# A three-layer graph network on one core: one product per pair for tiles 11 to 21, and 655 listed gathers a layer in place of 495

## The chip, the cores and the metric

The kernel runs on one core of one Trainium2 chip. The metric is the device time of one execution in microseconds (us). The engines are named as in the profile: PE (TensorE; PEld is its weight load), DVE (VectorE), ACT (ScalarE), POOL (GpSimd), SP (SyncE, which issues most DMAs). Each engine works through its own queue in order; an instruction that waits for a semaphore holds up everything behind it on that engine.

## The reference

6250 nodes with 128 features, 200,000 edges sorted by destination, destinations crowded towards low node numbers (6250·u², u uniform), sources uniform.

```python
def _sage_conv(x, src, dst, Wl, bl, Wr):
    agg = jax.ops.segment_max(x[src], dst, num_segments=x.shape[0])
    agg = jnp.where(jnp.isfinite(agg), agg, 0.0)
    return agg @ Wl + bl + x @ Wr
...
h = jnp.maximum(_layernorm(x, axis=-1), 0.0)
# three layers, 128 -> 256 -> 256 -> 128, each: h = leaky_relu(_sage_conv(h, ...), 0.01)
x = x + h
```

So for every node and layer the elementwise maximum over the rows of its in-neighbours is wanted, then two small matrix products.

## The kernel before

**Tiles and pairs.** The nodes stand in 50 tiles of 127. As sources, two tiles make a pair, so there are 25 pairs. As destinations, tiles 0 to 2, whose nodes have the most edges, are split into 8 "virtual" tiles whose rows have at most 64 edges each; the other 47 tiles stand for themselves. The destinations are in four groups (`GROUPS`, L94): group 0 is 20 tiles (30 to 49), group 1 the 8 virtual tiles, group 2 the 19 tiles 3 to 21, group 3 the 8 tiles 22 to 29.

**Products.** A neighbour's row is fetched by a matrix product: for a destination chunk and a source pair, a one-hot matrix (`one_hot`, L940: ACT, and in layer 0 DVE at L956 for some) picks one edge per destination node, PE multiplies it with the pair's rows kept as a high and a low half (`products`, L990), and DVE takes the maximum with the accumulator (`maxima`, L1007). A *narrow* destination tile ("n") takes one edge per pair: both source tiles of the pair add into one PSUM tile, then one maximum. A *wide* tile ("w") takes one edge per source tile: two PSUM tiles and two maxima. The matmuls are as many for either. Virtual tiles are wide and have beside that a second, narrow product per pair (`EXTRA`, "x", L100). A step is one chunk of one group against one pair: up to 8 tiles of columns in layer 0 (128 features), up to 4 in layers 1 and 2 (256 features). A full step has 8 matmuls of 512 columns.

**Lists.** Edges that find no place in a product are listed (`pick_rows`, `rank_rows`, `send_row`: up to 24 or 48 per node) and sorted by length, so that the q-th row of 128 nodes of a list needs at most `CAPS[k][q]` edges. In each layer class `Listed` (L1009) fetches them with indirect DMAs that POOL issues (`gather`, L1039), 128 rows each: 495 of them a layer, which is the sum of `CAPS`. ACT releases the indices (`let`, L1028) two steps ahead (`LEAD`), a ring of 8 tiles `g` takes the rows, DVE folds them (L1053, L1058), and SP stores the result in `best`.

**Order.** The steps of a layer are dealt into sweeps over the pairs (`SWEEPS`, L1179): layer 0 as groups (0), (1), (2 with 3); layer 1 as (0 with 1), (2 with 3); layer 2 as (0 with 1), (2), (3). The main loop (L1420) writes for each step t, to all engines' queues, what an agenda holds for t. For the gathers the agenda is made at L1278 to L1300: they are spread evenly over the steps from `t0` to `t1`, and the fold that needs them is planned `DELAY` = 8 or 6 steps later:

```python
        t0, t1 = max(b0 + 2, rows_at), end - 1 - SOON
...
                    plan(max(whens[i] - LEAD, 0), LET, lambda li=li, t=t: li.release(t))
                    plan(whens[i], GATHER, lambda li=li, t=t: li.gather(t))
                    at = max(at, whens[i] + (SOON if k == NL - 1 else DELAY[layer]))
                plan(at, MAXIMA, lambda li=li, t=t: li.maximum(t))
```

`rows_at` is the step by which the last tile's new rows are written: when a group's sweep and list are done, its tiles go one by one through class `Node` (L1065: an indirect DMA `agg` on POOL, transposes, the two products, the row stored into the next layer's table), and those of groups 2 and 3 fall into the first 33 steps of the next layer. No gather of a layer may run before its table is whole.

**Layer 0** carries besides that the making of the lists and of the one-hot indices for groups 1 to 3 ("chores": `late_rows` L1218, `late_lookups` L1237), spread over steps 0 to 82. 44 gathers (`EARLY`) of layer 0 are issued before the first step.

Of the kernel before, what the change touches and what calls it, by code (L numbers as in the profile page):

```python
# [42 lines left out]
P = 128  # L43
# [7 lines left out]
CB = 40  # L51
# [8 lines left out]
)  # L60
NEAR, FIRST = 20, 30
DEEP = (24, 24, 48, 24)
WINDOW = (48, 64)
# [6 lines left out]
def kernel(ctx: ExitStack, tc: tile.TileContext, x, src, dst,  # L70
# [31 lines left out]
    PLACE, HEAD = {}, []  # L102
    for units in GROUPS:
        HEAD.append(len(PLACE))
        for u in units:
            PLACE[u] = len(PLACE)
    NU = len(PLACE)

# [3 lines left out]

    TILES = [[tile_of(u) for u in units] for units in GROUPS]
    LISTS = GROUPS
    NL = len(LISTS)
# [28 lines left out]
    cols = dram.tile([P, T], I16, name="cols")  # L144
    IW = [(len(units) + sum(w == "w" for w, _ in units)) * P for units in PLANES]
# [3 lines left out]
    OW = [sum(w == "w" for w, _ in units) * P for units in PLANES]  # L149
    far = [dram.tile([P, NG, FW[k]], U8, name=f"far{k}") for k in range(len(GROUPS))]  # L150
# [356 lines left out]
    def flag_rows(us, S):  # L507
# [23 lines left out]
        one_less = slice(0, J - 1)  # L531
        if wide and us[0][1] >= NW:
# [17 lines left out]
    def pick_rows(k, i0, us, S):  # L550

        n, W, m = len(us), width_of(us), DEEP[k]
        whole = S(0, F32, n, W)
        nc.vector.tensor_copy(whole, rows_of(us)[:, :, :W])
        top = S(2, F32, n, m)
        for i in range(n):
            for o in range(0, m, 8):
                nc.vector.max(out=top[:, i, o : o + 8], in_=whole[:, i, :])  # L558
                if o + 8 < m:
                    nc.vector.match_replace(  # L560
                        out=whole[:, i, :], in_to_replace=top[:, i, o : o + 8], in_values=whole[:, i, :], imm_value=0.0
                    )
        nc.vector.tensor_scalar(picked[k][:, i0 : i0 + n, :], top, -float(LEAF), 0.0, op0=OP.add, op1=OP.max)
        there = S(0, F32, n, m)
        nc.vector.tensor_scalar(there, top, float(LEAF), None, op0=OP.is_ge)
        nc.vector.reduce_sum(left_n[k][:, i0 : i0 + n], there, axis=AX.X)

# [153 lines left out]
    def window_check():  # L721
        for i, (c0, c1, n) in enumerate(
            ((FIRST, NT, WINDOW[0]), (22, FIRST, WINDOW[1]), (VT, 22, 2 * CUT))
        ):
# [25 lines left out]
    def lookups(us, least, s, pool, tags=("v", "v8")):  # L750
# [9 lines left out]
        while i < n:  # L760
# [8 lines left out]
            nc.scalar.copy(part.rearrange("g (c k) -> g c k", k=P), p[:, :m, :])  # L769
            at = NV + PLANES[k].index(us[i]) if us[i] in EXTRA else GROUPS[k].index(us[i]) + (len(GROUPS[k]) if s else 0)  # L770
            nc.sync.dma_start(idx[k][:, at * P : (at + m) * P], part)
# [59 lines left out]
    list_consts()  # L831
    for i0 in (0, NEAR // 2):
        mask_rows(L0[i0 : i0 + NEAR // 2], S_first)
        flag_rows(L0[i0 : i0 + NEAR // 2], S_first)
        if i0:
# [3 lines left out]
            for i in range(NW):  # L839
                row(("w", i))  # L840
        pick_rows(0, i0, L0[i0 : i0 + NEAR // 2], S_first)
    rank_rows(0, S_first, first)
# [87 lines left out]
    def parts_of(k):  # L930

        units = PLANES[k]
        for w in "wnx":
            us = [i for i, u in enumerate(units) if u[0] == w]
            for i0 in range(0, len(us), HOT // P):
                yield us[i0], len(us[i0 : i0 + HOT // P]) * P, len(GROUPS[k]) if w == "w" else 0

    hots, gone, slots, turn_o = {}, {}, {}, [0]

    def one_hot(layer, k, g, c, w, odd, s):  # L940

# [6 lines left out]
        if layer == 0:  # L948
            at = of + (c + (odd if s else 0) + (NV if PLANES[k][c] in EXTRA else 0)) * P
        elif k == 0:  # L950
# [26 lines left out]
    def products(step, s, p):  # L977
# [3 lines left out]
        K = widths[layer] // P  # L981
        c0, pw, _ = next(q for q in parts_of(k) if q[0] <= c < q[0] + q[1] // P)
        hot = hots[layer, k, g, c0, s]
# [81 lines left out]
    class Node:  # L1065
# [28 lines left out]
        def merge(self):  # L1094
# [4 lines left out]
            self.m = node.tile([P, 2, P], F32, tag="mz", name="mz", bufs=2)  # L1099
            if self.k is None:  # L1100
                nc.vector.tensor_copy(self.m[:, :K, :], aT_p)
# [79 lines left out]
    for layer in range(3):  # L1181
        begins.append(len(steps))
        for ks in SWEEPS[layer]:
            for g in range(NG - 1, -1, -1):
                kinds = [[], []]
                for k in ks:
                    for c0, w, _ in parts_of(k):
                        part = [c for c in chunks(layer, k) if c0 <= c[2] < c0 + w // P]
# [29 lines left out]
    def late_rows(k):  # L1218
        us = LISTS[k]
        i0 = 0  # L1220
        for part in [us]:
            chores.append((2.5, lambda part=part: mask_rows(part, S_acc)))
            chores.append((18 if part[0][0] == "w" else 6, lambda part=part: flag_rows(part, S_acc)))
            for i in range(0, len(part), 4):
# [47 lines left out]
    for layer in range(3):  # L1272
# [6 lines left out]
        alone = len(SWEEPS[layer][-1]) == 1  # L1279
        for part, t0, t1 in (((lists_[:3], t0, turn), (lists_[3:], turn, t1)) if alone else ((lists_, t0, t1),)):  # L1280
# [3 lines left out]
            n = sum(len(li.seq) for li in part) - early  # L1284
# [6 lines left out]
        done_at, i, at = [], 0, 0  # L1291
        for k, li in enumerate(lists_):
            for t in range(len(li.seq)):
                if whens[i] is None:
                    at = 1 + i // 8
                else:
                    plan(max(whens[i] - LEAD, 0), LET, lambda li=li, t=t: li.release(t))
                    plan(whens[i], GATHER, lambda li=li, t=t: li.gather(t))
                    at = max(at, whens[i] + (SOON if k == NL - 1 else DELAY[layer]))
                plan(at, MAXIMA, lambda li=li, t=t: li.maximum(t))  # L1300
                i += 1
            done_at.append(at)
        gap = (2, 3, 3)[layer]
# [59 lines left out]
    for i, (layer, sweep, g) in enumerate(order):  # L1363
        for k in SWEEPS[layer][sweep]:
            for c, w, odd in parts_of(k):
                for s in range(2):
                    jobs_h.append((at_step[layer, k, g, c], i, (layer, k, g, c, w, odd, s)))
    jobs_h.sort(key=lambda j: j[0])
# [33 lines left out]
    for t in range(EARLY):  # L1402
        soon.release(t)
        soon.gather(t)
    least = first.tile([P, len(L0), NG], I16, name="least_a")
    for g0 in range(0, NG, BATCH):
        expand(L0, CB, g0, 0, least, S_first)
    lookups(L0, least, 0, first, ("xs0", "xs1"))
    load_layer(0, const, first)
# [4 lines left out]
    made = making.enter_context(tc.tile_pool(name="made", bufs=1, side="right"))  # L1414
    acc_t = [work.tile([P, 2, n * P], F32, name=f"acc{i}") for i, n in enumerate((NN, NV + NW))]
    ACC = ((0, 0), (1, 0), (1, NV), (0, NEAR))
    pair_until(0)
# [326 lines left out]
```

## Time and profile before

| | |
|---|---|
| median of 3 executions | 3248.2 us (3247.44 to 3262.78) |
| the profiled execution | 3258.48 us; span from first to last instruction 3256.5 us |
| mean granted TensorE clock | 0.921 |
| busy share PE / DVE / ACT / POOL | 75% / 84% / 58% / 57% |
| DMA | 571.20 MB, mean 175 GB/s |

Busy time is that of instructions at work; POOL's time for a DMA is that of writing its descriptors, and the rows land later. A group's mean is the time of one instruction. "Idle before, releaser" says what ended the idle time ahead of it.

### The profile page before, as it was taken

What the parts mean: (1) busy time and instruction counts of PE and PEld (TensorE: products, weight loads), DVE (VectorE), ACT (ScalarE), POOL (GpSimd) and SP (SyncE); (2) the same over time, 40 slices, a digit from 0 to 9 for tenths busy, and PEclk for the clock granted to TensorE, in tenths of its full rate; (3) what the DMA queues carried; (4) which work ended last, traced back from release to release, by engine and by line L of the source; (5) the groups of instructions that cost most, each with busy time, mean ns of one, the idle gap of its engine ahead of it and who ended that gap; (6) DMA issues with size and microseconds to landing.
All of it is one profiled execution on the core that took longest, in us unless ns stands there. A gap on an engine that the chain in (4) does not pass through costs nothing.

```text
span 3256.5 us, 37116 instructions
## 1 busy us (share of the span) xinstructions
PE 2448.4 (75%) x9919; PEld 1785.3 (55%) x9920; DVE 2740.2 (84%) x4320; ACT 1901.7 (58%) x2753; POOL 1862.4 (57%) x1885
## 2 busy tenths in 40 slices
PE   1025622448777779999988888889999997878787
PEld 1023311235444457777765655567777775655566
DVE  6677899987999987899986799995799897999965
ACT  4127942646867656666654566655666664555553
POOL 4787523446777742766664455532466665654563
PEclk9996865678999999999999999999999998999999
DMA  9234521339866767666766655656666575655586
GB/s 305 59 66 139 150 68 33 110 99 242 241 185 194 183 189 230 199 208 201 204 167 192 203 165 177 171 154 212 206 197 203 180 179 181 201 166 159 155 258 182
DMA packets 358250, 571.20 MB, mean 175 GB/s; under 512 B 65270, under 2 KB 213379, under 8 KB 357393
## 3 DMA queue, kind: packets, MB, share of 16 engines
q1 hardware_dynamic: 237201, 341.17, 32.7%
q0 software_dynamic: 77568, 193.35, 23.6%
q10 hardware_dynamic: 43264, 34.21, 3.2%
q8 instruction: 83, 1.36, 0.2%
q14 instruction: 134, 1.10, 0.1%
HBM read 443.95 MB, written 124.54 MB: 175 GB/s over the span
## 4 chain that ended last, share of the span: by engine, by line
PE 36%; DVE 29%; DMA 12%; issue 9%; POOL 5%; ACT 4%; SPq 1%; DVEq 0%; ACTq 0%; POOLq 0%
PE pg L990 28%; DVE acc L1007 13%; POOL g L1039 5%; DMA g<-table,let 4%; PE z_p L1111 3%; DVE g L1058 3%; PE z_p L1113 2%; DVE g L1053 2%; ACT hot L962 2%; ACT away L960 2%; DMA pair_sb<-pair 2%; DVE acc L742 1%; DVE acc L560 1%; DVE acc L558 1%; DVE acc L736 1%
## 5 line engine op out<-in xcount | busy, mean ns | idle before, releaser
L990 PE MATMUL pg<-hot,pair_sb 128*128 128x512 f32 (+1 forms) x8000 | 2150.7, 417 | 411.2 <-ACT hot L962 126.4
L1039 POOL DMA_INDIRECT g<-table,let x1485 | 1510.7, 1017 | 929.1 <-ACT let L1028 359.9
L990 PEld LDWEIGHTS pg<-hot,pair_sb 128*128 128x128 f32 x8000 | 1507.6, 199 | 925.8 <-ACT hot L962 236.8
L1007 DVE TENSOR_TENSOR acc<-acc,pg 128x1024 f32<-128x1024 f32 (+3 forms) x1439 | 1638.3, 1166 | 278.4 <-PE pg L990 251.3
L962 ACT ACTIVATE hot<-away 128x1024 fp32r<-128x1024 uint8 (+2 forms) x600 | 573.9, 957 | 405.8 <-PE pg L990 391.8
L962 ACT ACTIVATE hot<-idx_sb 128x1024 fp32r<-128x1024 uint8 (+2 forms) x600 | 555.0, 937 | 230.3 <-PE pg L990 216.0
L960 ACT ACTIVATE away<-idx_sb,near 128x1024 uint8<-128x1024 uint8 (+2 forms) x600 | 620.4, 1034 | 56.7 <-DMA idx_sb<-idx 25.8
L1082 POOL DMA_INDIRECT agg<-best,end_i x141 | 141.1, 1001 | 236.2 <-PE aT_p L1098 190.6
L1115 ACT COPY s<-z_p 127x256 f32<-127x256 f32 (+1 forms) x150 | 50.3, 335 | 308.1 <-PE z_p L1113 258.4
L1053 DVE TENSOR_TENSOR g<-g 128x1024 f32<-128x1024 f32 (+5 forms) x211 | 206.6, 979 | 10.8 <-DMA g<-table,let 10.7
L1058 DVE TENSOR_TENSOR g<-g 128x256 f32<-128x256 f32 (+3 forms) x357 | 175.5, 492 | 10.6 <-DVE g L1053 0.2
L1111 PE MATMUL z_p<-wr,hT_in 128*128 128x256 f32 (+1 forms) x500 | 136.3, 390 | 1.0 <-DMA hT_in<-across 0.9
L1028 ACT ACTIVATE let<-ell 128x4 int32<-128x4 int16 (+3 forms) x435 | 78.5, 190 | 92.8 <-DMA ell<-picks 82.6
L1113 PE MATMUL z_p<-wl,mz 128*128 128x256 f32 (+1 forms) x500 | 119.7, 356 | 12.2 <-DVE mz L1104 11.4
L624 POOL DMA_INDIRECT picks<-picked,to_i x55 | 56.8, 1032 | 120.9 <-DVE rank_h L600 90.4
L1104 DVE TENSOR_TENSOR mz<-acc,aT_p 128x256 f32<-128x256 f32 (+1 forms) x141 | 52.5, 372 | 72.7 <-PE aT_p L1098 72.7
L956 DVE TENSOR_SCALAR hot<-idx_sb,beyond 128x1024 fp32r<-128x1024 uint8 (+1 forms) x150 | 108.5, 723 | 0.0
L1113 PEld LDWEIGHTS z_p<-wl,mz 128*128 128x128 f32 x500 | 88.6, 203 | 23.8 <-DVE mz L1104 13.8
L1111 PEld LDWEIGHTS z_p<-wr,hT_in 128*128 128x128 f32 x500 | 80.9, 204 | 33.8 <-issue 11.5
L867 ACT COPY hT<-hT_p 128x254 f32<-128x254 f32 x100 | 36.9, 369 | 80.5 <-PE hT_p L865 80.4
L354 POOL DMA_INDIRECT win_d<-in_dst_dram,win_i x50 | 54.2, 1084 | 46.6 <-ACT junk_w L359 18.0
L767 PE MATMUL lk_p<-ident_b,v 128*25 128x128 bf16 x90 | 10.5, 285 | 87.9 <-DVE v L755 59.4
(281 smaller groups left out, 1212.6 us busy)
## 6 DMA issues: line engine op xcount, KB each, us to landing
pair_sb<-pair SPq DMA_DIRECT2D x325, 256.0 KB
idx_sb<-far SPq DMA_DIRECT2D x50, 640.0 KB
far<-away ACTq DMA_DIRECT2D x225, 128.0 KB
pair<-pr SPq DMA_DIRECT2D x100, 256.0 KB
g<-table,let POOLq DMA_INDIRECT x1485
idx_sb<-idx SPq DMA_DIRECT2D x25, 608.0 KB
idx_sb<-far SPq DMA_DIRECT2D x50, 304.0 KB
idx_sb<-idx SPq DMA_DIRECT2D x50, 304.0 KB
```

What stands on the lines that cost most here:

```text
L956: nc.vector.tensor_scalar(hot[:, :w], d, beyond, None, op0=OP.is_equal)
L960: nc.scalar.activation(away, d, AF.Abs, bias=near[:, s : s + 1], scale=1.0)
L962: nc.scalar.activation(hot[:, :w], d, AF.Relu, bias=1.0, scale=-1.0)
L990: nc.tensor.matmul(to, pr[:, i, kk * P : (kk + 1) * P], hot[:, o : o + bw], start=((alone or s == 0) and i == 0), stop=((alone or s == 1) ...
L1007: nc.vector.tensor_max(to, to, of)
L1028: nc.scalar.activation(let[:, :n], ell[self.k][:, q, j : j + n], AF.Identity, scale=1.0)
L1039: nc.gpsimd.indirect_dma_start(out=self.tiles[q, b][:, i, :], out_offset=None, in_=tables[self.layer], in_offset=bass.IndirectOffsetOnAxis ...
L1053: nc.vector.tensor_max(base[:, : i + 1, :], base[:, : i + 1, :], g[:, : i + 1, :])
L1058: nc.vector.tensor_max(base[:, :h, :], base[:, :h, :], base[:, w - h : w, :])
L1082: nc.gpsimd.indirect_dma_start(out=self.agg[:, : self.F], out_offset=None, in_=of, in_offset=bass.IndirectOffsetOnAxis(ap=at, axis=0),)
L1111: nc.tensor.matmul(z_p, self.hT[:, i, :], wr[layer][:, i, :], start=False, stop=False)
L1113: nc.tensor.matmul(z_p, self.m[:, i, :], wl[layer][:, i, :], start=False, stop=(i == K - 1))
```

## The change

Three things are changed, the rest follows from them.

Only tiles 3 to 10 stay wide. Tiles 11 to 21 become narrow: 11 to 17 form group 3 (7 tiles), 18 to 29 go behind the wide ones in group 2 (8 + 12 tiles). The virtual tiles lose their second, narrow product (`EXTRA` is empty); the edges that it took are listed. So `CAPS` grows to 655 gathers a layer (118 + 172 + 255 + 110, before 118 + 70 + 230 + 77), and `DEEP`, how many edges a row of a list may have, from 24, 24, 48, 24 to 24, 40, 48, 40.

The steps become 200 + 350 + 350 = 900, before 225 + 400 + 400 = 1025. By sweep, before and after:

| sweep (layer: groups) | steps | L990 matmuls | maxima from PSUM | gathers planned |
|---|---|---|---|---|
| 0: 0 | 75, 75 | 500, 500 | 75, 75 | 152, 232 |
| 0: 1 | 50, 25 | 400, 200 | 75, 50 | 103, 79 |
| 0: 2 and 3 | 100, 100 | 700, 700 | 175, 125 | 196, 300 |
| 1: 0 and 1 | 225, 175 | 1800, 1400 | 275, 225 | 249, 299 |
| 1: 2 and 3 | 175, 175 | 1400, 1400 | 300, 225 | 246, 356 |
| 2: 0 and 1 | 225, 175 | 1800, 1400 | 275, 225 | 241, 293 |
| 2: 2 | 125, 125 | 1000, 1000 | 250, 175 | 188, 266 |
| 2: 3 | 50, 50 | 400, 400 | 50, 50 | 66, 96 |

(The plan; 44 gathers of layer 0 stand before step 0.) In layer 2 the list of group 3 is now cut in two: its first part is gathered ahead of group 2's list, so that the gathers come evenly over both sweeps. `LISTED` = 0 changes nothing.

```diff
 CAPS = (
     (22, 10, 9, 8, 8, 7, 6, 6, 6, 5, 5, 4, 4, 4, 3, 3, 3, 2, 2, 1),
-    (21, 12, 10, 9, 7, 5, 4, 2),
-    (47, 24, 20, 17, 15, 13, 12, 11, 10, 9, 8, 8, 7, 6, 6, 5, 5, 4, 3),
-    (23, 12, 10, 9, 7, 6, 5, 5),
+    (37, 28, 25, 22, 20, 17, 13, 10),
+    (47, 25, 21, 18, 16, 14, 13, 12, 11, 11, 10, 9, 8, 8, 7, 7, 6, 5, 4, 3),
+    (34, 18, 15, 13, 12, 10, 8),
 )
-NEAR, FIRST = 20, 30
-DEEP = (24, 24, 48, 24)
+NEAR, FIRST, MID, HI = 20, 30, 18, 11
+DEEP = (24, 40, 48, 40)
+NARROWLY = (24, 0, 32, 40)
...
-    WIDE = list(range(VT, 22))
-    NARROW = list(range(FIRST, NT)) + list(range(22, FIRST))
+    WIDE = list(range(VT, HI))
+    NARROW = list(range(FIRST, NT)) + list(range(MID, FIRST)) + list(range(HI, MID))
+    BOTH = NEAR + FIRST - MID
     GROUPS = (
-        [("n", i) for i in range(NEAR)],
+        [("n", i) for i in range(NP)],
         [("w", NW + v) for v in range(NV)],
-        [("w", i) for i in range(NW)],
-        [("n", i) for i in range(NEAR, NN)],
+        [("w", i) for i in range(NW)] + [("n", i) for i in range(NEAR, BOTH)],
+        [("n", i) for i in range(BOTH, NN)],
     )
-    EXTRA = [("x", v) for v in range(NV)]
+    EXTRA = []
...
-    late_lookups(EXTRA, 0)
     n_soon = len(chores)
     late_rows(2)
-    for i0, i1 in ((0, 7), (7, 13), (13, 19)):
-        for s in range(2):
-            late_lookups(LISTS[2][i0:i1], s)
+    for s in range(2):
+        late_lookups(LISTS[2][:NW], s)
+    rest2 = LISTS[2][NW:]
+    cuts = -(-len(rest2) // 8)
+    for i in range(cuts):
+        late_lookups(rest2[len(rest2) * i // cuts : len(rest2) * (i + 1) // cuts], 0)
...
+        items = [(k, t) for k in range(NL) for t in range(len(lists_[k].seq))]
+        if alone:
+            own = [(3, t) for t in range(len(lists_[3].seq))]
+            later_n = len(items) * (t1 - turn) / (t1 - t0)
+            heads = [t for t, (_, j) in enumerate(lists_[3].seq) if j == 0]
+            cut = min(heads, key=lambda t: abs(len(own) - t - later_n))
+            mid = next(i for i, (k, _) in enumerate(items) if k == 2)
+            items = items[:mid] + own[:cut] + [q for q in items if q[0] == 2] + own[cut:]
```

More of the change, by code (lines that the diff above doesn't have):

```diff
@@ L144 @@
     cols = dram.tile([P, T], I16, name="cols")
-    IW = [(len(units) + sum(w == "w" for w, _ in units)) * P for units in PLANES]
+    ODD = [sum(w == "w" for w, _ in units) for units in PLANES]
+    IW = [(len(units) + ODD[k]) * P for k, units in enumerate(PLANES)]
     idx = [dram.tile([NG, IW[k]], U8, name=f"idx{k}") for k in range(len(GROUPS))]
@@ L148 @@
     FW = [DW[k] // (2 if k else 1) for k in range(len(GROUPS))]
-    OW = [sum(w == "w" for w, _ in units) * P for units in PLANES]
+    OW = [n * P for n in ODD]
     far = [dram.tile([P, NG, FW[k]], U8, name=f"far{k}") for k in range(len(GROUPS))]
@@ L531, in flag_rows @@
         one_less = slice(0, J - 1)
-        if wide and us[0][1] >= NW:
+        if EXTRA and wide and us[0][1] >= NW:
             c, seen = S(1, I32, n, J), S(2, I32, n, J)
@@ L1220, in late_rows @@
         i0 = 0
-        for part in [us]:
+        for part in [list(p) for _, p in itertools.groupby(us, key=lambda u: u[0])]:
             chores.append((2.5, lambda part=part: mask_rows(part, S_acc)))
-            chores.append((18 if part[0][0] == "w" else 6, lambda part=part: flag_rows(part, S_acc)))
+            chores.append((len(part) * (1 if part[0][0] == "w" else .6), lambda part=part: flag_rows(part, S_acc)))
             for i in range(0, len(part), 4):
@@ L1279 @@
         alone = len(SWEEPS[layer][-1]) == 1
-        for part, t0, t1 in (((lists_[:3], t0, turn), (lists_[3:], turn, t1)) if alone else ((lists_, t0, t1),)):
+        items = [(k, t) for k in range(NL) for t in range(len(lists_[k].seq))]
[6 more added lines that the diff above has]
+            items = items[:mid] + own[:cut] + [q for q in items if q[0] == 2] + own[cut:]
+            parted = len(items) - (len(own) - cut)
+        for part, t0, t1 in (((items[:parted], t0, turn), (items[parted:], turn, t1)) if alone else ((items, t0, t1),)):
             total = [0.0]
@@ L1283 @@
                 total.append(total[-1] + (WIDER[layer] if steps[t][3][3] is not None else 1.0))
-            n = sum(len(li.seq) for li in part) - early
+            n = len(part) - early
             whens += [None] * early
@@ L1290 @@
                 whens.append(t0 + t)
[L1291 to L1302, printed above, removed]
+        done_at, at = [0] * NL, 0
+        for i, (k, t) in enumerate(items):
+            li = lists_[k]
+            if whens[i] is None:
+                at = 1 + i // 8
+            else:
+                plan(max(whens[i] - LEAD, 0), LET, lambda li=li, t=t: li.release(t))
+                plan(whens[i], GATHER, lambda li=li, t=t: li.gather(t))
+                at = max(at, whens[i] + (SOON if k == NL - 1 and not (alone and i < parted) else DELAY[layer]))
+            plan(at, MAXIMA, lambda li=li, t=t: li.maximum(t))
+            done_at[k] = at
         gap = (2, 3, 3)[layer]
@@ L1364 @@
         for k in SWEEPS[layer][sweep]:
-            for c, w, odd in parts_of(k):
+            for c, w in parts_of(k):
                 for s in range(2):
-                    jobs_h.append((at_step[layer, k, g, c], i, (layer, k, g, c, w, odd, s)))
+                    jobs_h.append((at_step[layer, k, g, c], i, (layer, k, g, c, w, s)))
     jobs_h.sort(key=lambda j: j[0])
@@ L1414 @@
     made = making.enter_context(tc.tile_pool(name="made", bufs=1, side="right"))
-    acc_t = [work.tile([P, 2, n * P], F32, name=f"acc{i}") for i, n in enumerate((NN, NV + NW))]
-    ACC = ((0, 0), (1, 0), (1, NV), (0, NEAR))
+    acc_t = [work.tile([P, 2, n * P], F32, name=f"acc{i}") for i, n in enumerate((NP + len(GROUPS[3]), NV + len(GROUPS[2])))]
+    ACC = ((0, 0), (1, 0), (1, NV), (0, NP))
     pair_until(0)
```

56 lines of the change are left out of this document (30 added, 26 removed).

## The prediction

> **What bounds the kernel now.** I read the busy shares first, then the windows cut at the first and last matmul of each sweep (found by counting the 8000 matmuls of L990 along the order of steps), then the groups, POOL's waits, and last the timeline.
>
> ```profile
> span 3256.5 us, 37116 instructions
> ## 1 busy us (share of the span) xinstructions
> PE 2448.4 (75%) x9919; PEld 1785.3 (55%) x9920; DVE 2740.2 (84%) x4320; ACT 1901.7 (58%) x2753; POOL 1862.4 (57%) x1885
> ```
>
> By the shares DVE leads and POOL has 43% to spare. Both are averages, and the second is misleading, as the windows and the timeline show. Columns of the windows: length, then busy time and number of instructions of PE, PEld, DVE, ACT and POOL, clock, DMA share, GB/s.
>
> ```profile
> 0.00:230.30 230.30, 34.34 (x148) 27.43 (x149) 155.34 (x603) 62.43 (x151) 153.93 (x171) 1.00 0.50 147
> 230.30:685.40 455.10, 206.37 (x574) 128.18 (x574) 390.68 (x1070) 283.85 (x356) 221.33 (x242) 0.68 0.37 100
> 685.40:899.00 213.60, 154.62 (x575) 104.01 (x576) 185.65 (x321) 134.89 (x196) 141.32 (x141) 0.87 0.76 208
> 899.00:1183.50 284.50, 206.08 (x741) 135.99 (x739) 269.64 (x374) 193.45 (x269) 215.77 (x204) 0.94 0.66 188
> 953.00:1171.00 218.00, 160.49 (x569) 104.93 (x568) 208.58 (x291) 149.94 (x208) 169.46 (x160) 0.94 0.68 194
> 1183.70:1298.00 114.30, 107.98 (x482) 78.42 (x483) 76.45 (x130) 68.25 (x129) 22.30 (x24) 0.97 0.65 213
> 1298.00:1664.50 366.50, 359.37 (x1537) 284.34 (x1536) 339.00 (x330) 252.91 (x333) 256.13 (x255) 1.00 0.69 202
> 1664.50:2185.20 520.70, 429.78 (x1732) 307.90 (x1730) 441.54 (x479) 300.55 (x447) 275.76 (x276) 0.95 0.59 177
> 2185.50:2317.70 132.20, 131.37 (x617) 100.65 (x618) 78.89 (x123) 67.06 (x126) 21.65 (x23) 1.00 0.61 197
> 2317.70:2692.90 375.20, 361.89 (x1536) 286.69 (x1535) 337.71 (x328) 252.13 (x331) 248.27 (x246) 0.99 0.67 196
> 2692.90:3082.70 389.80, 312.69 (x1286) 220.72 (x1284) 357.64 (x402) 208.19 (x310) 219.19 (x220) 0.93 0.55 168
> 3082.70:3226.80 144.10, 127.85 (x609) 97.79 (x609) 98.20 (x140) 75.39 (x104) 79.22 (x79) 0.96 0.81 245
> 3226.80:3256.50 29.70, 16.05 (x93) 13.06 (x92) 9.04 (x28) 2.12 (x8) 7.55 (x8) 0.79 0.37 103
> ```
>
> Rows one to four are the set-up and layer 0: DVE is at 86%, 87% and 95%. Row five lies inside row four. Rows six to eight are layer 1: first the 33 steps into which the last tiles of layer 0 fall, with hardly a gather and PE at 94%; then PE at 98%; then DVE at 85% and PE at 83%, in turns. Rows nine to twelve are the same for layer 2 (131 of 132 us PE; PE 96%; DVE 92%; PE 89%), and the last row is the tail. So today PE and DVE share the end, POOL follows.
>
> ```profile
> L990 PE MATMUL pg<-hot,pair_sb 128*128 128x512 f32 (+1 forms) x8000 | 2150.7, 417 | 411.2 <-ACT hot L962 126.4
> L1039 POOL DMA_INDIRECT g<-table,let x1485 | 1510.7, 1017 | 929.1 <-ACT let L1028 359.9
> ...
> L1007 DVE TENSOR_TENSOR acc<-acc,pg 128x1024 f32<-128x1024 f32 (+3 forms) x1439 | 1638.3, 1166 | 278.4 <-PE pg L990 251.3
> ...
> L1053 DVE TENSOR_TENSOR g<-g 128x1024 f32<-128x1024 f32 (+5 forms) x211 | 206.6, 979 | 10.8 <-DMA g<-table,let 10.7
> L1058 DVE TENSOR_TENSOR g<-g 128x256 f32<-128x256 f32 (+3 forms) x357 | 175.5, 492 | 10.6 <-DVE g L1053 0.2
> ```
>
> Now POOL's own waits: us in total, times, longest.
>
> ```profile
> POOL g L1039 <- ACT let L1028: 359.9, 140, 27.1
> POOL g L1039 <- issue: 341.2, 1108, 3.3
> POOL agg L1082 <- PE aT_p L1098: 191.6, 59, 24.1
> POOL g L1039 <- DVE acc L1007: 107.2, 92, 15.0
> POOL picks L624 <- DVE rank_h L600: 90.4, 1, 90.4
> ```
>
> The second row is the one that matters: 1108 times POOL stood 0.31 us before a gather although nothing was owed to it. The timeline shows this as a fixed 0.30 us ahead of each:
>
> ```profile
> 1001.02 0.94 POOL L1039 DMA_INDIRECT g<-table,let  x1 [0.30 <-ACT hot L962]
> ...
> 1003.88 0.41 DVE L1053 TENSOR_TENSOR g<-g 128x256 f32<-128x256 f32 x1
> 1003.95 1.16 POOL L1039 DMA_INDIRECT g<-table,let  x1 [0.30 <-issue]
> 1004.33 1.48 DVE L1058 TENSOR_TENSOR g<-g 128x512 f32<-128x512 f32 x3
> ```
>
> A gather thus takes POOL not 1.017 but some 1.3 us: 0.94 + 0.30 = 1.24 at its best, 1.16 + 0.30 where folds of the ring run beside it. And from 953 to 1171 us POOL is full already: 160 instructions in 218.0 us, 1.36 us each, with a busy share of only 169.46/218 = 78%. A POOL that shows 78% has nothing left.
>
> **Part by part.**
>
> *Taken from PE.* 1000 of the 8000 matmuls go (200 in layer 0, 400 in each other layer): 1000 x 2150.7/8000 = 269 us.
>
> *Taken from DVE.* Maxima from PSUM fall from 1475 (1439 and 36 first copies) to 1150: 325 x 1.166 = 379 us. The folds grow with the gathers: (206.6 + 175.5)/1485 = 0.257 us each, 480 x 0.257 = 123 us. The chores shrink, below.
>
> *Taken from the chores.* These are the rows of layer 0's first sweep alone:
>
> ```profile
> L742 DVE TENSOR_TENSOR acc<-acc 128x960 int16<-128x960 int16 (+2 forms) x135 | 66.8, 495 | 4.6
> L736 DVE TENSOR_SCALAR acc<-rows_w 128x384 int16<-128x384 int16 (+2 forms) x200 | 47.4, 302 | 0.3
> L558 DVE MAX8 acc<-acc 128x8 f32<-128x128 f32 (+1 forms) x146 | 38.6, 277 | 4.3
> L560 DVE MATCH_REPLACE8 acc<-acc,acc 128x128 f32<-128x128 f32 (+1 forms) x116 | 30.5, 263 | 0.0
> ```
>
> Lookups (L736, L742) go over 62 planes of 64 columns and 8 of 40, together 4288; after it are 32 and 19, 2808. So 35% of 114 us, 39 us. The picks (L558, L560) go from 162 rounds of eight to 171, though fewer on 128-wide rows: nothing either way.
>
> *Added to POOL.* 160 gathers a layer. The price of one lies between 1.24 us (the best case) and 1.36 us (the crowded stretch). Two rows place it between: the mean of L1039 in the last sweep of layer 0 and in the last of layer 1.
>
> ```profile
> L1039 POOL DMA_INDIRECT g<-table,let x191 | 203.5, 1065 | 58.2 <-issue 46.3 <-DMA g<-table,let 4.6 <-DVE acc L1007 1.8
> ```
>
> ```profile
> L1039 POOL DMA_INDIRECT g<-table,let x243 | 243.8, 1003 | 213.0 <-ACT let L1028 125.6 <-issue 52.4 <-DVE acc L1007 24.5
> ```
>
> With 0.30 ahead of each that is 1.365 and 1.30. I take 1.35 in layer 0 and 1.31 in layers 1 and 2, a little over 1.30 because a third more folds will run beside the gathers. The other indirect DMAs on POOL (node rows, list rows) are of the same kind and get the same price, an estimate.
>
> The page "SBUF — State Buffer" of the Trainium skill (Who interferes with whom) says that a `tensor_tensor` with both inputs in SBUF meets only GpSimd's reads, and infers that it does not hold up descriptor writing. By that the folds would lengthen no gather, and the sum would be that of the first rival, 3211 us of span; this trace has 1.16 us beside folds, against 0.94, so the measurement decides.
>
> *The sum goes by POOL.* Gathers are dealt evenly over the steps and each step's folds wait for theirs, so when POOL needs more time for a step's gathers than PE and DVE need for the step, POOL sets the pace.
>
> Layer 0: the three windows hold 242 + 141 + 204 = 587 POOL instructions; plus 160 is 747, of which 35 are the short memsets ahead of the list rows (0.3 us of gap and little more, 15 us together, an estimate). 712 x 1.35 + 15 = 976 us, against the 953 us that these sweeps take now. POOL also stands before a list's rows until DVE has ranked it (90.4 us now); DVE has less to do ahead of that, and a fold may lag 8 steps, so I leave 30 us. With 12 us for the five steps behind the last gather: 230 + 976 + 30 + 12 = 1248 us, now 1183.
>
> Layer 1: the 33 steps without gathers keep 27 tiles, 8 matmuls a step and so their 114 us. Then 255 + 276 + 160 = 691 instructions x 1.31 = 905 us, and 12. Together 1031; now 1002.
>
> Layer 2: 132, then 246 + 220 + 79 + 160 = 705 x 1.31 = 924, then 12 and the tail of 30. Together 1098; now 1071.
>
> Without POOL the stretch of layer 1's first sweep behind the 33 steps would take 142 steps of now 193, PE 359.37 x 142/193 = 264 us; its 299 gathers take POOL 392. In the second sweep DVE falls to 441.54 - 75 x 1.166 + 110 x 0.257 = 382, PE stays at 430, POOL has 356 gathers and about 30 others: 506. So the relief of PE and DVE comes to nothing: POOL's queue covers it. ACT, under 70% in these windows, gains and costs nothing. DMA neither: the fullest window, the last sweep, has a share of 0.81 at 245 GB/s, 35 MB; its 30 further gathers, 128 rows of 1 KB each, are 4 MB.
>
> Sum: 1248 + 1031 + 1098 = 3377 us of span, 3379 as a time (the profiled execution has 3258.48 on a span of 3256.5). That execution lies 10 us over the median of 3248.2. **Forecast: 3370 us.**
>
> **Rivals.**
>
> *Gathers at their best price (ends on the other side).* If POOL, once full, went at 1.245 us, layer 0 would end at 230 + 712 x 1.245 + 15 + 42 = 1173, layer 1 take 114 + 860 + 12 and layer 2 132 + 878 + 42: 3211 of span, about 3203 as a median, 1.4% faster. For it: the row of 0.94, with a maximum from PSUM beside it as DVE's commonest work. Against it: both group means, and the full stretch at 1.36. It decides below a mean of (3256 - 3377)/2108 = 0.057 us under my 1.324, so at 1.267. Chance 0.16.
>
> *Gathers hidden altogether.* If the further gathers fitted into the 43% that POOL idles by its share, today's bounds would count: 400 matmuls less in each of two PE-bound sweeps (2 x 400 x 0.269 = 215 us), 150 maxima less and 188 gathers' folds more in two DVE-bound ones (175 - 48 = 127), and in layer 0 75 maxima (87) and 39 of chores less, 160 folds (41) more, so 85: 3256 - 427, a median near 2820. Against it: 0.94 us of POOL and a gap of 0.30 for every gather. Chance 0.04. The Trainium skill speaks for this rival: its page "DMA: Bandwidth & Descriptors" (Anatomy of one DMA, the SWDGE path) calls descriptor generation small and puts most of a DMA's fixed cost into its completion, which many gathers in flight would share; the 0.94 us on POOL's own track does not agree.
>
> *POOL full, and waiting besides.* The 107.2 us that gathers waited behind DVE are a full ring of 8 tiles. With 1965 gathers in place of 1485 that would be 142 us, none of it hidden any more: 3377 + 142, a median near 3510. Against it: POOL met the full ring because it ran ahead, and a POOL that is last doesn't; from 953 to 1171 us 169.46 of work and 160 gaps of 0.30 fill 217.5 of the 218.0 us and leave no room for it. Chance 0.14.
>
> *The lists overflow.* If a sorted list were longer than `CAPS` says, the kernel would take its general path, 1573 gathers in each of three layers one after the other, over 3 x 1573 x 1.24 = 5.9 ms. Nothing in the profile speaks for it. Chance 0.01.
>
> **How the numbers follow.** The forecast gets the remaining 0.65: prices of 1.27 to 1.36 us make 3255 to 3445 of it. The range reaches from 3190, into the best-price case, to 3480, into the case of waits; outside lie 0.04 + 0.01 and about a third of the two others. What can be told from no change is 0.5%, 16 us. Faster: 0.04, four fifths of 0.16, so 0.17. Within 0.5%: the lower end of the forecast's prices and the rest of that rival, 0.08. Slower: 0.75.
>
> **What would show it.** Right: 1965 gathers and POOL busy about 70% of the span, (1862 + 480 x 1.02)/3377, with nearly every idle time before a gather 0.30 us; "POOL g <- ACT let" down from 359.9 us to under 100; the maxima of L1007 1114 times and L990 7000; in the first sweeps of layers 1 and 2, behind the 33 steps, PE near 264/392 = 67% in place of 98 and 96%, in their second sweeps DVE near 382/506 = 75%, and DVE waiting for landed gathers; those 33 steps still 114 and 132 us. Wrong: a mean of L1039 under 0.96 us (the best price), or POOL still waiting hundreds of us for `let` (POOL is not the bound), or long waits of gathers behind DVE's L1007 (the ring). If layer 0 ends before 1183 us, its sum is wrong.

## The result, and the profile after

The kernel after takes **3424.6 us** (median of 4, 3417.92 to 3429.15) beside 3255.49 us (3247.44 to 3265.47, 4) for the kernel before on the same chip: **1.0516 times** as long, 95% interval 1.0475 to 1.0558. The forecast was 3370 us. The profiled execution took 3429.15 us on a span of 3427.2.

The first four experiments below ran on another chip, on which the kernel before takes 3564.68 us and the change was not run; their ratios stand beside that time only.

The head of the page and the shares of the chain that ended last, by line:

```profile
span 3427.2 us, 35225 instructions
## 1 busy us (share of the span) xinstructions
PE 2323.1 (68%) x8901; PEld 1714.6 (50%) x8901; DVE 2432.9 (71%) x3966; ACT 1704.0 (50%) x2670; POOL 2368.9 (69%) x2365
...
DMA g<-table,let 17%; POOL g L1046 14%; PE pg L997 13%; DVE acc L1014 8%; DVE g L1060 3%; PE z_p L1118 2%; DVE g L1065 2%; PE z_p L1120 2%; DMA agg<-best,end_i 2%; ACT away L967 2%; ACT hot L969 2%; DMA joined<-joined_v 1%; DVE acc L560 1%; DMA pair_sb<-pair 1%; DVE acc L558 1%
```

No engine shows over 71%, and yet the kernel is longer: PE and DVE lost work (125 and 307 us), POOL gained 506.5 us. The landing of the gathers and their issue now head the chain with 17% and 14%, before it was 4% and 5%. The windows, cut as in the prediction (columns: length, then busy time and count of PE, PEld, DVE, ACT and POOL, clock, DMA share, GB/s):

```profile
0.00:229.20 229.20, 34.57 (x149) 27.45 (x149) 154.94 (x604) 62.45 (x151) 154.28 (x171) 0.90 0.49 147
229.20:665.90 436.70, 215.71 (x563) 132.21 (x564) 346.71 (x1025) 290.87 (x383) 294.71 (x322) 0.65 0.44 117
665.90:816.00 150.10, 102.73 (x366) 68.93 (x364) 118.86 (x203) 70.09 (x124) 112.69 (x115) 0.79 0.83 224
816.00:1229.10 413.10, 232.34 (x743) 169.30 (x744) 254.12 (x353) 203.16 (x304) 315.59 (x310) 0.76 0.54 140
1229.10:1344.00 114.90, 110.22 (x492) 79.76 (x491) 80.48 (x134) 64.75 (x128) 22.65 (x23) 0.98 0.70 226
1344.00:1726.30 382.30, 300.31 (x1128) 226.77 (x1127) 291.51 (x285) 178.19 (x271) 294.15 (x290) 0.91 0.63 184
1726.30:2286.50 560.20, 431.91 (x1732) 328.23 (x1730) 393.15 (x434) 304.29 (x473) 415.37 (x401) 0.89 0.66 193
2286.50:2423.20 136.70, 134.30 (x622) 102.49 (x623) 84.37 (x128) 64.71 (x126) 21.77 (x23) 0.99 0.65 207
2423.20:2808.20 385.00, 302.33 (x1132) 230.85 (x1131) 290.93 (x286) 178.54 (x270) 296.06 (x287) 0.88 0.63 184
2808.20:3211.10 402.90, 313.81 (x1287) 233.06 (x1286) 307.16 (x350) 213.80 (x328) 304.20 (x294) 0.89 0.64 188
3211.10:3390.60 179.50, 128.61 (x621) 102.39 (x619) 101.92 (x148) 71.33 (x113) 130.79 (x127) 0.90 0.81 228
3390.60:3427.20 36.60, 16.27 (x82) 13.12 (x81) 8.70 (x26) 1.86 (x7) 6.63 (x7) 0.65 0.29 80
```

Take the sixth row, the first sweep of layer 1 behind the 33 steps: POOL shows 294.15 us of 382.30, 77%. Add a gap of 0.305 us for each of its 290 instructions, 88 us, and it is full: 382.6. PE is at 79%, DVE at 76%. The seventh row: 415.37 + 401 x 0.305 = 537.7 of 560.2. Of the gather windows of layers 1 and 2 (1344.0 to 2286, 2423.3 to 3391), POOL stood idle beyond that fixed gap for 23.0 and 11.9 us. The timeline, POOL's instructions alone (start, length, idle before and releaser):

```profile
1480.22 0.95 POOL L1046 DMA_INDIRECT g<-table,let  x1 [0.30 <-DVE acc L1014]
1481.48 0.95 POOL L1046 DMA_INDIRECT g<-table,let  x1 [0.30 <-issue]
1482.73 0.94 POOL L1046 DMA_INDIRECT g<-table,let  x1 [0.30 <-ACT let L1035]
```

The releasers named differ; the gap is 0.30 whichever is named. By the trace, 98% of the 1965 gathers stand 0.31 us or less behind the instruction before them; in the kernel before it was 87%. The groups, and the waits (total, times, longest):

```profile
L1046 POOL DMA_INDIRECT g<-table,let x1965 | 2012.7, 1024 | 700.7 <-issue 477.6
L997 PE MATMUL pg<-hot,pair_sb 128*128 128x512 f32 (+1 forms) x7000 | 2020.2, 442 | 655.0 <-DVE acc L1014 307.3
...
L1014 DVE TENSOR_TENSOR acc<-acc,pg 128x1024 f32<-128x1024 f32 (+2 forms) x1114 | 1285.4, 1178 | 301.2 <-PE pg L997 287.2
...
L1060 DVE TENSOR_TENSOR g<-g 128x1024 f32<-128x1024 f32 (+4 forms) x312 | 325.5, 1043 | 338.2 <-DMA g<-table,let 314.0
...
L1065 DVE TENSOR_TENSOR g<-g 128x512 f32<-128x512 f32 (+3 forms) x362 | 181.5, 502 | 49.3 <-DMA g<-table,let 31.6
```

```profile
POOL g L1046 <- issue: 477.6, 1540, 8.4
POOL agg L1089 <- PE aT_p L1105: 155.4, 53, 15.9
POOL picks L630 <- DVE rank_h L606: 41.8, 1, 41.8
POOL g L1046 <- DVE acc L1014: 39.9, 131, 0.3
POOL g L1046 <- ACT let L1035: 36.4, 43, 9.2
DVE g L1060 <- DMA g<-table,let: 314.0, 116, 18.1
PE pg L997 <- DVE acc L1014: 307.3, 131, 14.1
```

PE's wait for DVE in the kernel before:

```profile
PE pg L990 <- DVE acc L1007: 113.5, 131, 14.1
```

POOL's 359.9 us behind `let` have gone to 36.4; in their place DVE waits 314.0 us for gathers that have not landed (10.7 before), and PE 307.3 us for DVE (113.5 before). So DVE now waits for POOL's gathers, and PE waits for DVE.

### The profile page after: what moved, and what is told of

It reads as the page before. It is cut to its first block, busy times and chain, and to the rows that moved or that the text cites. A ratio compares the mean times of both kernels' runs of the same rounds, so it can differ in the third digit from the quotient of the medians.

```text
span 3427.2 us, 35225 instructions
## 1 busy us (share of the span) xinstructions
PE 2323.1 (68%) x8901; PEld 1714.6 (50%) x8901; DVE 2432.9 (71%) x3966; ACT 1704.0 (50%) x2670; POOL 2368.9 (69%) x2365
## 3 DMA queue, kind: packets, MB, share of 16 engines
q14 instruction: 137, 1.12, 0.1%
## 4 chain that ended last, share of the span: by engine, by line
DMA 24%; PE 20%; DVE 20%; POOL 16%; issue 12%; ACT 4%; SPq 0%; DVEq 0%; ACTq 0%; POOLq 0%
DMA g<-table,let 17%; POOL g L1046 14%; PE pg L997 13%; DVE acc L1014 8%; DVE g L1060 3%; PE z_p L1118 2%; DVE g L1065 2%; PE z_p L1120 2%; DMA agg<-best,end_i 2%; ACT away L967 2%; ACT hot L969 2%; DMA joined<-joined_v 1%; DVE acc L560 1%; DMA pair_sb<-pair 1%; DVE acc L558 1%
## 5 line engine op out<-in xcount | busy, mean ns | idle before, releaser
L1046 POOL DMA_INDIRECT g<-table,let x1965 | 2012.7, 1024 | 700.7 <-issue 477.6
L997 PE MATMUL pg<-hot,pair_sb 128*128 128x512 f32 (+1 forms) x7000 | 2020.2, 442 | 655.0 <-DVE acc L1014 307.3
L997 PEld LDWEIGHTS pg<-hot,pair_sb 128*128 128x128 f32 x7000 | 1438.4, 215 | 1104.2 <-issue 232.8
L1014 DVE TENSOR_TENSOR acc<-acc,pg 128x1024 f32<-128x1024 f32 (+2 forms) x1114 | 1285.4, 1178 | 301.2 <-PE pg L997 287.2
L969 ACT ACTIVATE hot<-away 128x1024 fp32r<-128x1024 uint8 (+2 forms) x525 | 494.4, 942 | 522.9 <-PE pg L997 511.4
L969 ACT ACTIVATE hot<-idx_sb 128x1024 fp32r<-128x1024 uint8 (+2 forms) x550 | 503.9, 928 | 372.9 <-PE pg L997 355.3
L1060 DVE TENSOR_TENSOR g<-g 128x1024 f32<-128x1024 f32 (+4 forms) x312 | 325.5, 1043 | 338.2 <-DMA g<-table,let 314.0
L967 ACT ACTIVATE away<-idx_sb,near 128x1024 uint8<-128x1024 uint8 (+2 forms) x525 | 535.0, 1019 | 48.3 <-DVE acc L491 15.4
L1065 DVE TENSOR_TENSOR g<-g 128x512 f32<-128x512 f32 (+3 forms) x362 | 181.5, 502 | 49.3 <-DMA g<-table,let 31.6
L1105 PE MATMUL aT_p<-ident,agg 128*128 128x128 f32 x250 | 57.7, 299 | 96.7 <-DMA agg<-best,end_i 74.4
L630 POOL DMA_INDIRECT picks<-picked,to_i x55 | 57.6, 1047 | 55.2 <-DVE rank_h L606 41.8
```

The costliest lines, as they stand in the source:

```text
L967: nc.scalar.activation(away, d, AF.Abs, bias=near[:, s : s + 1], scale=1.0)
L969: nc.scalar.activation(hot[:, :w], d, AF.Relu, bias=1.0, scale=-1.0)
L997: nc.tensor.matmul(to, pr[:, i, kk * P : (kk + 1) * P], hot[:, o : o + bw], start=((alone or s == 0) and i == 0), stop=((alone or s == 1) ...
L1014: nc.vector.tensor_max(to, to, of)
L1046: nc.gpsimd.indirect_dma_start(out=self.tiles[q, b][:, i, :], out_offset=None, in_=tables[self.layer], in_offset=bass.IndirectOffsetOnAxis ...
L1060: nc.vector.tensor_max(base[:, : i + 1, :], base[:, : i + 1, :], g[:, : i + 1, :])
```

## The experiments

**Theory 1**: POOL sets the pace. Its indirect DMAs cost some 1.33 us each, and the 480 further gathers use up what room it had and then lengthen the kernel. **Theory 2**: the cost lies in the change's form (narrow tiles, new lists, pacing). Further rivals were that landing latency or the folds' own time is what is paid.

### On the other chip: the halves, and fewer gathers

e1: the change with the second products and the old list of group 1 put back (553 gathers a layer).

```diff
-    (37, 28, 25, 22, 20, 17, 13, 10),
+    (21, 12, 10, 9, 7, 5, 4, 2),
-DEEP = (24, 40, 48, 40)
+DEEP = (24, 24, 48, 40)
-    EXTRA = []
+    EXTRA = [("x", v) for v in range(NV)]
...
+    late_lookups(EXTRA, 0)
```

> The changed kernel with the virtual tiles' second product put back and their list as before: 118 + 70 + 255 + 110 = 553 gathers a layer, so only the narrow tiles 11 to 21 of the change are in. Theory 1, POOL's queue at 1.33 us an indirect DMA: in layers 1 and 2 POOL needs about (553 + 31) x 1.33 = 777 us behind the 33 steps, less than the 887 us of the old stretch, so it holds nothing up there; the second sweeps, DVE-bound before, lose 75 maxima each. Sum about 1190 + 946 + 1018 = 3154 us, so 3100 to 3200, FASTER than before. Theory 2, the narrow tiles themselves cost time (their longer lists wait on landing, or PE at a lower granted clock): slower than before, 3300 or more.

e2: the reverse, the kernel before with `EXTRA = []`, `CAPS[1]` and `DEEP[1]` as in the change (597 gathers a layer).

> The kernel before with the second product of the virtual tiles taken out and their edges listed: 118 + 172 + 230 + 77 = 597 gathers a layer, tiles 11 to 21 still wide. Theory 1, POOL's queue: layer 0 POOL-bound at about 970 us behind the set-up; first sweeps of layers 1 and 2 at 115 + 344 and 137 + 344 us with POOL and PE near each other, second sweeps as before or POOL-bound, 525 and 405; sum about 3275 us, so 3220 to 3330, near the time before. Theory 2, what decides is the work on PE and DVE (1000 matmuls and 125 maxima go): faster than before by over 200 us, under 3050.

e3: the change with the second products put back and its lists kept (655 gathers). The diff is e1's last two edits.

> The changed kernel with the virtual tiles' second product put back although the lists keep their 655 gathers a layer (the further places stay empty and fetch the floor row): 1000 matmuls, 125 maxima and 150 one-hots more on engines that theory 1 calls idle. Theory 1, POOL's queue covers it: 3390 to 3480 us, as the changed kernel within 2%, with POOL still at gaps of 0.30 us. Theory 2, PE, DVE or the clock decide: 1000 x 0.289 us of PE or 150 us of DVE and 290 us of ACT come on top, 3560 to 3700.

e4: the change, with only 495 of the 655 gathers a layer issued: `Listed` goes by a shorter table `RUN` in place of `CAPS`.

```diff
+RUN = (
+    CAPS[0],
+    (22, 16, 14, 13, 11, 10, 8, 6),
+    (37, 20, 16, 14, 13, 11, 10, 9, 9, 8, 8, 7, 7, 6, 6, 5, 5, 4, 3, 2),
+    (24, 12, 11, 9, 8, 7, 6),
+)
...
-            self.seq = [(q, j) for q, m in enumerate(CAPS[k]) for j in range(m)]
+            self.seq = [(q, j) for q, m in enumerate(RUN[k]) for j in range(m)]
```

> The changed kernel, all products as they are, but the lists of groups 1 to 3 are fetched only as far as 100, 200 and 77 rows, so 495 gathers a layer as before; edges beyond that are left out of the maximum. Theory 1: layer 0 ends near 1095, layer 1 takes 875, layer 2 957: 2890 to 2980 us, and POOL waits for let again by hundreds of us. Theory 2, the landing of gathers or the DMA volume decides: each gather fewer is worth its bytes only (480 x 0.13 MB at 175 GB/s at most, 360 us if nothing hides it, none if all is hidden): 3065 to 3425. Theory 3, the lower clock decides: 3350 or more.

Measured beside 3564.68 us: e1 3661.32 (1.0281, 1.0233 to 1.0328), e2 3856.6 (1.0826, 1.077 to 1.0882), e3 4079.22 (1.1433, 1.1394 to 1.1472), e4 3374.12 (0.9454, 0.9409 to 0.95). The order of the four fits theory 1, the sizes don't (e1 came out slower than the kernel before, where theory 1 had it faster and theory 2 slower), and the change, against which e3 and e4 were to be read, has no time here. This chip also waits where the first one did not. The maxima of the same 495-gather kernel, here and in e10 further down:

```profile
L1020 DVE TENSOR_TENSOR acc<-acc,pg 128x1024 f32<-128x1024 f32 (+2 forms) x1114 | 1289.8, 1180 | 712.9 <-PE pg L1003 313.1 <-remote 285.0 <-issue 86.7
```

```profile
L1020 DVE TENSOR_TENSOR acc<-acc,pg 128x1024 f32<-128x1024 f32 (+2 forms) x1114 | 1282.8, 1178 | 263.2 <-PE pg L1003 247.6
```

The instructions take as long (1180 and 1178 ns); 285.0 us of the idle time are put down to `remote`, a releaser that the profile doesn't find on this core, and 3374 us stand against 2883. PE, DVE and ACT stand idle together for 337 us here and 89 in e10, by the traces; in e1 to e4 it is 319 to 515 us, not the 200 to 400 that the expectation of e5 below gives. What the cause is stays open. All were run again on chips where the kernel before takes what it did at first.

### The change once more, and its first half

> The changed kernel as it is, for a chip where it stands beside the others of this call. The four runs before this were on a chip on which the kernel before takes 3564.68 us, with all of PE, DVE and ACT idle together for 200 to 400 us; their ratios can only be set against the changed kernel on the same chip. Theory 1 (POOL's queue): 1.04 to 1.06 of the kernel before where that takes about 3255 us; about 1.10 to 1.13 where it takes 3565. Theory 2 (what costs is the state of that chip, not the queue): the ratio is 1.05 on any chip.

e5, the change itself: 3425.13 us beside 3256.11, 1.0524 (1.0495 to 1.0554). The cost stands.

> Narrow tiles 11 to 21 alone, 553 gathers a layer, the second product of the virtual tiles back: the kernel of e1 beside the changed kernel. Theory 1: on a chip where the kernel before takes about 3255 us, 3100 to 3200, a ratio of 0.95 to 0.985, with POOL waiting for let by over 200 us; under the changed kernel by 200 us or more on any chip. Theory 2, the narrow tiles cost time: a ratio of 1.01 or more, as e1 had it (1.028).

e6, the kernel of e1: **3154.52 us, 0.9694 (0.9667 to 0.9721)**: the narrow tiles by themselves, with 58 more gathers a layer, gain 102 us. It is the fastest version that does the whole work, and beats both kernels. Theory 2's form (narrow tiles, two-part list, pacing) is all in it. Two of its windows, the sweeps of layer 1:

```profile
1275.60:1667.50 391.90, 365.51 (x1529) 287.77 (x1527) 349.63 (x342) 252.58 (x344) 300.79 (x289) 0.98 0.69 200
1667.50:2119.40 451.90, 403.92 (x1731) 309.55 (x1731) 365.47 (x405) 300.12 (x446) 306.01 (x299) 0.96 0.70 210
```

In the first, PE is at 93% and POOL with its gaps (300.79 + 289 x 0.305 = 388.9) at 99%: both are nearly full. In the second, PE and POOL (306.01 + 299 x 0.305 = 397.2) are at 89% and 88%.

### The second half

> The second half by itself: tiles 11 to 21 stay wide as in the kernel before, the virtual tiles lose their second product, CAPS[1] and DEEP[1] as in the change, 597 gathers a layer (the kernel of e2). Theory 1 (POOL sets the pace, 1.30 to 1.34 us for each of its indirect DMAs, once these need longer than PE and DVE): 102 gathers a layer more than before would take POOL 306 x 1.32 = 404 us; before, POOL stood some 360 us for released indices, most of which is used up by it; and 200 maxima fewer do not help where POOL is last. 3220 to 3330 us. Theory 2 (what costs is the change's order of gathers and lists, not their number): this kernel has the order of before, so no slower than before, 3100 to 3240 us.

e9, the kernel of e2: 3341.11 us beside 3253.38, 1.0274 (1.0255 to 1.0293), 11 us over theory 1's range, and theory 2 (not slower, the old order being kept) falls. So the halves give -102 and +88, together -14, and the change +169. They don't add, and that is the clue: both draw on the same idle time of POOL, which the account below counts.

### The second products back, at the same 655 gathers

> The changed kernel with the virtual tiles' second product put back and the 655 gathers a layer kept: the kernel of e3 beside the changed kernel. Theory 1, POOL's queue covers the added work: within 2% of the changed kernel, 3390 to 3490 us where that takes 3425. Theory 2, PE, DVE, ACT or the clock decide: 4 to 8% over the changed kernel.

e7, the kernel of e3: 3540.77 us, 1.0881 (1.0853 to 1.0909), 115.6 us or 3.4% over the change. Neither theory's figure. POOL's work is the same, 2371.5 us in 2365 instructions; what grew is its idle time, for one in a row that stands at 33.6 us in the change:

```profile
POOL g L1046 <- DMA g<-table,let: 93.1, 164, 2.9
```

Of these 93.1 us, 164 gaps of 0.305 are 50; beyond them 43 us are left, in the change 3. Counted from the first to the last gather of each layer, POOL is idle beyond its gap for 195 us, in the change for 96. So a POOL that sets the pace isn't wholly deaf to the work beside it: with more work on PE, DVE and ACT it loses 99 us here. By the trace, 42 of them lie in waits under 2 us, and 31 in the two waits for the ranks of layer 0's lists (52.9 and 24.0 us, in the change 41.8 and 3.7).

### Fewer gathers

> The change with its products, sweeps and order, but only 495 of its 655 gathers a layer are issued (the last ones of each row of a list are left out, and with them the edges that they fetch; the kernel of e4). Theory 1: 160 gathers a layer fewer at 1.31, 1.335 and 1.335 us would be 637 us off a POOL that is always last; PE and DVE then bound in several sweeps, so 2890 to 2980 us, clearly below the kernel before, which issues as many. Theory 2 (the narrow tiles, the two-part list and the new pacing cost by themselves): not faster than before, 3250 us or more.

e10, the kernel of e4: 2882.55 us, 0.8856 (0.8839 to 0.8874), 7 us under theory 1's range.

> As e10, but 575 of the 655 gathers a layer are issued; the edges of the other 80 are left out. Theory 1: POOL stays last in nearly all sweeps, so 80 x (1.31 + 2 x 1.335) = 318 us less than the change at most: 3105 us, range 3060 to 3140, and the step from 575 to 495 is worth less than that from 655 to 575, since PE and DVE come up as bounds in between. Theory 3 (a gather costs only by its landing and fold, DVE 0.257 us and a wait, POOL has room): 80 x 3 x 0.257 = 62 us, 3360 us.

e11, by the same edit with 575 issued: 3150.51 us, 0.9687 (0.967 to 0.9704), 11 us over theory 1's range. Theory 2 falls with e10, theory 3 (a gather costs a fold) with e11. The steps are 3425.13 - 3150.51 = 275 and 3150.51 - 2882.55 = 268 us for 240 gathers each: 1.14 and 1.12 us a gather, nearly straight. (3425.13 is from the comparison of e5, where the kernel before takes 3 us more.) I had expected the second step to be the smaller; it hardly is. The windows of e10, the same two sweeps of layer 1:

```profile
1196.00:1493.10 297.10, 271.27 (x1127) 207.67 (x1126) 269.99 (x268) 175.48 (x252) 229.05 (x224) 0.99 0.69 208
1493.10:1942.20 449.10, 402.51 (x1732) 306.84 (x1730) 366.41 (x412) 300.95 (x451) 311.81 (x306) 0.97 0.69 213
```

Even at 495 gathers POOL is full in the first: 229.05 + 224 x 0.305 = 297.4 of 297.1 us, with PE and DVE at 91%. In the second, POOL (311.81 + 306 x 0.305 = 405.1) and PE are both at 90%. So at 495 gathers PE and DVE come near POOL, and in the second sweep PE is level with it; POOL still gained idle time by as much in either step, 53 and 45 us by the table of the account.

### The folds, and the landing

e8: the change without its two folds of the ring.

```diff
-                nc.vector.tensor_max(base[:, : i + 1, :], base[:, : i + 1, :], g[:, : i + 1, :])
...
-                    nc.vector.tensor_max(base[:, :h, :], base[:, :h, :], base[:, w - h : w, :])
```

It leaves out most listed edges.

> The changed kernel without DVE's folds of the gathered rows (the two lines with tensor_max in maximum): all 1965 gathers are issued, but only the first row of each list goes into the result, so the rest of the listed edges is left out. It takes away 500 us of DVE work and what that does to gathers beside it. Theory 1, POOL's queue sets the time and the folds lengthen gathers: L1046 falls from 1.024 to about 0.96 us, so 2108 x 0.065 = 140 us less, 3270 to 3320 where the changed kernel takes 3425. Theory 2, POOL sets the time but the folds have no part in a gather's length: no change, 3410 to 3440. Theory 3, DVE sets the time: 300 to 500 us less, 2950 to 3100.

Measured: 3276.12 us, 1.006 (1.004 to 1.0081), 149 us less than the change, with 140 expected. The gathers:

```profile
L1046 POOL DMA_INDIRECT g<-table,let x1965 | 1887.6, 961 | 705.4 <-issue 499.9 <-DMA g<-table,let 55.1 <-DMA pair<-pr 52.8
```

961 ns each in place of 1024: 125 us less of POOL's busy time at the same count, of the 149 gained. DVE went from 2432.9 to 1973.8 us, three times the gain. So the folds are paid in the main through POOL. The change's own trace has the same: the 663 gathers beside which DVE ran nothing but maxima from PSUM took 0.948 us on average, the 600 with a fold beside them 1.151. The Trainium skill's page "SBUF — State Buffer" (Who interferes with whom) infers that a `tensor_tensor` from SBUF doesn't hold up descriptor writing; the 63 ns disagree for these gathers. But they also read their indices from SBUF, and for GpSimd's reads the page does name contention; no run here separates the two.

e12: the change, with later folds.

```diff
-    DELAY = (8, 6, 6)
+    DELAY = (12, 9, 9)
```

> The change with DELAY = (12, 9, 9) in place of (8, 6, 6): a fold may come 12 or 9 steps after its gather. Theory 1: POOL's queue is full of gathers, and when their folds come changes neither their number nor their price: 3425 us, plus or minus 20. Rival (the 314 us in which DVE waits for landed gathers are landing latency that a longer lead would hide): 100 to 300 us less.

Measured: 3431.29 us, 1.054 (1.0522 to 1.0559), no change. DVE waits for landed gathers as long as before:

```profile
L1060 DVE TENSOR_TENSOR g<-g 128x1024 f32<-128x1024 f32 (+4 forms) x312 | 325.1, 1042 | 342.8 <-DMA g<-table,let 309.9 <-issue 30.7 <-DMA agg<-best,end_i 1.8
```

The waits are not latency that a longer planned lead hides. They last 2.7 us on average in the change (314.0 us over 116), less than the 3.6 us that the page has as the median between a gather's issue and its landing:

```profile
g<-table,let POOLq DMA_INDIRECT x1965, 3.6
```

So on average DVE comes to a fold when its gather is issued and not yet landed. That POOL runs behind its plan, so that the planned lead isn't there when the fold comes, would explain why more steps don't help; that POOL hardly waits for its indices any more (36.4 us behind `let`) fits, but no run measures it.

### The account

With POOL's idle time beyond the gap of 0.305 us added up over each kernel's gather windows, every time can be laid out as gathers added (at 1.33 us, the change's price in layer 1) minus idle time used up:

| | gathers, three layers | POOL idle | 1.33 x added - used up | measured |
|---|---|---|---|---|
| before | 1485 | 562 us | | |
| e10, the change's products, 495 | 1485 | 194 | 0 - 368 = -368 | -371 |
| e6, first half | 1659 | 219 | 231 - 343 = -112 | -102 |
| e11, 575 issued | 1725 | 149 | 319 - 413 = -94 | -103 |
| e9, second half | 1791 | 217 | 407 - 345 = +62 | +88 |
| e7, second products back | 1965 | 195 | 638 - 367 = +271 | +285 |
| the change | 1965 | 96 | 638 - 466 = +172 | +169 |

The windows are made up of POOL's work, its gaps and its idle time, so in the main this is book-keeping, with one price for all and up to 26 us (e9) over. What the runs add is how much idle time each kernel uses up. Before, POOL had 562 us to give. The change's lighter products alone are worth 371 us (e10). Its 480 gathers take back 540.

## Why the prediction was right, and where it was off

**The mechanism was right.** "The sum goes by POOL" is what windows, waits, e10, e11 and e12 show. The 50 us of span that it lacks (3427.2 against 3377) come from its terms. Layer 0 came out 19 us shorter than forecast, layers 1 and 2 were 26 and 43 us longer; that these partly cancel is luck.

*Layer 0* ends at 1229, not 1248. The price of 1.35 us was too high: the 710 indirect DMAs took 718.4 us and their gaps 212.3, so 1.311 each, 28 us less in all, and the short memsets took 4.7 us where 15 were put. The price came from the most crowded row of before (1.065 + 0.30); that DVE has less to do beside the gathers now would fit, but is not shown to be the reason. Against that, POOL's idle time and the end behind its last DMA took 65 us where 42 were left, 41.8 of it the one wait for the ranks.

*Layer 1* took 1057 us, not 1031, and *layer 2* with the tail 1141, not 1098. Here 1.31 was too low: (709.5 + 210.0)/690 = 1.333 and (730.1 + 214.5)/705 = 1.340. That is the term of the sum that was sized too small, by some 16 and 21 us. It allowed 0.01 for a third more folds; e8 shows 0.063 us for all the folds, and the row it was read from (1003 ns) stood at 1038:

```profile
L1046 POOL DMA_INDIRECT g<-table,let x366 | 379.9, 1038 | 134.4 <-issue 85.7 <-ACT let L1035 16.1 <-DVE acc L1014 10.7
```

This is the second sweep of layer 1. The rest is POOL's waits, the second gather-less window (136.7 us, not 132) and the tail (36.6, not 30).

**"The relief of PE and DVE comes to nothing" was too strong.** e7 prices one part of it, the second products, at 116 us even with POOL full. The chain of reasoning that only the largest engine counts gives the sum here to within 2%, and leaves out what POOL loses in waits between steps.

**The signs looked for.** Seen as said: 7000 matmuls, 1114 maxima, POOL at 69%, a gap of 0.30, `let` at 36.4 us, DVE waiting for landed gathers, the first gather-less window 114.9 us. DVE's account came out too: -307 us where -379 - 39 + 123 = -295 was worked out, with the folds at +125. Off: in the first sweep PE stands at 79%, not 67%, since a matmul took 300.31/1128 = 0.266 us, before 359.37/1537 = 0.234, at a granted clock of 0.91 instead of 1.00. The clock alone would give 0.257, an estimate; the rest stays open. It didn't matter, as POOL set the end. (The old stretch has 1536 matmuls, so 192 steps and not 193; that moves the 67% to 68%.) DVE in the second sweep stands at 70%, not 75%, the window being longer.

**The rivals.** Gathers at 1.245 us: the layers stand at 1.311, 1.333 and 1.340; e8, without folds, has 0.961 + 0.30 = 1.26 and is still 0.6% slower than before, so that even this price would not have brought the gain of 1.4%. Hidden gathers: each step of 80 a layer costs 270 us. POOL full and waiting: the waits behind the maxima fell from 107.2 to 39.9 us, where that rival had 142, and these are 131 times the bare gap of 0.30. The lists didn't overflow; the gathers are 1965.

## What to carry to other kernels

Before work is moved to an engine with a low share, count its instructions in its busiest window and add the fixed gap of each: a POOL at 77% was full. Then ask how much idle time is left in all: two changes that use up the same idle time can cost more together than one by one (-102 and +88 made +169). Here the first alone was the better kernel, 3154.52 us.

## What the runs showed of the hardware

POOL's gathers of 128 rows follow the instruction before them with a gap of 0.30 us that no wait explains: it is 0.305 us in the median of each of the 14 traces. Their length depends on what DVE does beside them: 0.94 us at best, 1.024 on average with the folds, 0.961 without. And the same kernel can differ from chip to chip: the kernel before took 3564.68 us in one comparison and 3253 to 3256 in the three others, on other chips, and the 495-gather kernel 3374 and 2883, with the same lengths of DVE's maxima and 285 us of their idle time put down to a releaser that the profile doesn't find on the core. Whether it was the chip or something beside it stays open.
